# LN1's turned tokens by way of DRAM, in a float32 conditional transformer block on one core

## The chip, the cores and the metric

The kernel runs on one core of a Trainium2 chip. A core has TensorE (PE in the profile: matmuls into PSUM; PEld are its weight loads), VectorE (DVE), ScalarE (ACT), GpSimd (POOL) and SyncE (SP), which here issues nearly all transfers between DRAM and SBUF, the on-chip memory of 128 partitions. Each engine works its own list of instructions in order; semaphores hold an instruction back until what it needs is there. The metric is device time in microseconds, the median of several executions. One execution is also recorded by the hardware profiler; its span runs from the first to the last instruction.

## The reference

Two sequences of 2048 tokens, 512 wide, pass through one block, conditioned on a vector per sequence. Cut to what matters:

```python
emb = jnp.dot(jax.nn.silu(t), ada_w) + ada_b
shift_msa, scale_msa, gate_msa, shift_mlp, scale_mlp, gate_mlp = jnp.split(emb, 6, axis=-1)
norm = _ln(x) * (1.0 + scale_msa[:, None]) + shift_msa[:, None]
h = jax.nn.gelu(jnp.dot(norm, ssm_w1) + ssm_b1, approximate=False)
ssm_out = jnp.dot(h, ssm_w2) + ssm_b2
x = x + gate_msa[:, None] * ssm_out
norm2 = _ln(x) * (1.0 + scale_mlp[:, None]) + shift_mlp[:, None]
hf = jax.nn.gelu(jnp.dot(norm2, ff_w1) + ff_b1, approximate=True)
ff_out = jnp.dot(hf, ff_w2) + ff_b2
x = x + gate_mlp[:, None] * ff_out
```

`ssm_w1` and `ssm_w2` are 512 x 512, `ff_w1` is 512 x 1024 and `ff_w2` 1024 x 512. All of it is float32.

## The kernel before, in words

**Tiling.** The 4096 tokens are cut into 8 blocks of 512 (`NBLK`, `TB`); a block is 1 MB. Blocks 0 to 3 are the first sequence, 4 to 7 the second. The products are done by Strassen's scheme in its Winograd form: an operand is cut in quarters, `first` and `second` (lines 398 and 405) make sums of quarters on VectorE or GpSimd, and seven products take the place of eight, gathered in PSUM banks.

**Stages of a block.** `norm1` (line 562) loads x, normalises each token, turns the block so that channels lie on partitions, scales and shifts it (`modulate`, line 532, four ScalarE instructions) and makes the sums of quarters for the first product (`norm1_sums`, line 542). `ssm1` (line 632) is that product with GELU; `ssm2` (line 675) the second one, added onto x in place and stored to `x1_d` in DRAM. `norm2` (line 598) normalises and turns the result for the feed-forward part and stores it to `turned_d` in DRAM; `tokens` (line 803) reads it back. `ff1` (line 813) and `ff2` (line 899) are the feed-forward part, two blocks at a time. Between them `weight_fw1` (line 722) reads `ff_w1`, makes its sums of quarters and stores them to `fw1_d`, from where `ff1` loads them.

**Turning a block.** `normed` (line 548) takes statistics, normalises (ScalarE) and transposes 32 x 32 squares (`turn`, line 527, VectorE) into one of two buffers in the region `far`, `blocks`. What remains is to exchange groups of 32 partitions. For LN1 that is `move` (line 556): sixteen transfers from SBUF to SBUF of 64 KB each, from 32 partitions of `blocks` to 32 partitions of `turned[i]`. Only after all four transposes can any of them start. Blocks 0 and 1 don't go this way: they are turned on TensorE (`turn_rows`, `rows_normed`), so LN1 by `move` is there for blocks 2 to 7. For LN2, `norm2` writes four times 256 KB into DRAM, each from 32 partitions, at the rows where they belong. In the profile both the moves and these writes are called `turned<-far`; the sizes, 64 and 256 KB, tell them apart.

**Buffers.** `turned[i]` lies in one of two places, by i mod 2, so LN1 of block i may write it only when `ssm1(i - 2)` has read it. `xs[i]` has five places, by i mod 5.

**Order of the work.** The code lists the operations in the order of their data: block i+3's `norm1`, then `ssm2(i)`, `norm2(i)`, `ssm1(i+2)` (lines 1130 to 1141). Class `Plan` (line 18) then fixes the order of each engine's instructions before the program is built. Each operation has a cost on each engine that may do it and a latency. TensorE's order is that of the code. `order` (line 84) works back from TensorE's matmuls to a due time for every operation (`late`); `simulate` (line 107) plays the program forward and gives each free engine, among the operations that can start, the one due soonest. So an engine's order rests on when the plan believes data to be there. On the chip an engine whose next instruction isn't ready waits, with all that stands behind it.

**The plan's DMA.** A transfer takes 640 ns to issue (`ISSUE`). One over 32 KB shares one pipe: it ends at the later of start + 1300 ns (`FLIGHT`) and the pipe's end, plus its bytes at 370 bytes per ns (`RATE`), plus 700 ns (`LANDING`). It may start only when the pipe's end is less than 4000 ns off (`BACKLOG`). For due times, an operation is due its smallest latency plus its bytes at `RATE`, plus 70 ns, before what needs it; `dma` (line 303) has a latency of 2000 ns, and `move` passes one of 2000 + 16 x 640 ns. All transfers of the program but four go by SP's queue, line 308. The framework under the kernel gives each transfer one of the semaphores set aside for DMA in turn, and a transfer whose semaphore is still in use by an earlier one waits at the head of its queue; the old plan doesn't reckon with it.

Of the kernel before, what the change touches and what calls it, by code (L numbers as in the profile page):

```python
# [20 lines left out]
class Plan:  # L21
# [8 lines left out]
    ISSUE, FLIGHT, LANDING, RATE, BACKLOG = 640.0, 1300.0, 700.0, 370.0, 4000.0  # L30
    RATED, LANDED = 0.5, 4000.0
    LITTLE = 1 << 15
    AHEAD, SLACK = 2500.0, 150.0

    def __init__(self, nc):
# [71 lines left out]
    def simulate(self):  # L107
        ops, hop = self.ops, self.HOP
        left, ready = [len(op.deps) for op in ops], [0.0] * len(ops)
        free = dict.fromkeys("pvags", 0.0)  # L110
        self.lock, pipe, holder = 0.0, 0.0, None
        tensor = [op for op in ops if op.engs == "p"]
        at, pools, found = 0, {e: [] for e in "vags"}, {}
        done = [False] * len(ops)

        def enter(op):
            if op.lead and op.late < 1e8:
                ready[op.n] = max(ready[op.n], op.late - op.lead)
            for e in op.engs:
                if e != "p":  # L120
                    pools[e].append(op)
                    found.pop(e, None)

        def choose(e):
            pool = pools[e]
            if not pool:
                return None
            at = {}
            for op in pool:
                wait = self.lock if e in op.shared else pipe - self.BACKLOG if op.size > self.LITTLE else 0.0  # L130
                at[op.n] = max(free[e], ready[op.n], wait)
            now = min(at.values())

            def rank(op):
                return op.late + (self.AHEAD if e == "v" and len(op.engs) > 1 else 0.0), op.n

            op = min((op for op in pool if at[op.n] <= now), key=rank)
            end = now + op.cost[e]
            soon = [u for u in pool if now < at[u.n] < end - self.SLACK and u.late < min(end, op.late)]
            if soon:  # L140
                op = min(soon, key=lambda u: (at[u.n], u.n))
            return at[op.n], op

        for op in ops:
            if not op.deps:
                enter(op)
        count = len(ops)
        while count:
            best = None
            if at < len(tensor) and not left[tensor[at].n]:  # L150
                best = (max(free["p"], ready[tensor[at].n]), -1.0, "p", tensor[at])
            for e in "avgs":
                if e not in found:
                    found[e] = choose(e)
                c = found[e]
                if c and (best is None or (c[0], c[1].late) < best[:2]):
                    best = (c[0], c[1].late, e, c[1])
            start, _, e, op = best
            op.on, op.start, op.after = e, start, None
            free_at, free[e] = free[e], start + op.cost[e]  # L160
            if op.size > self.LITTLE:
                pipe = max(start + self.FLIGHT, pipe) + op.size / self.RATE * (1 + self.RATED * op.care)
                op.end = pipe + self.LANDING + self.LANDED * op.care
                found.pop("a", None), found.pop("s", None)
            else:
                op.end = start + op.lat[e]
                if op.size and e == "s":
                    op.end = max(op.end, pipe + self.LANDING)
            if e in op.shared:
                if e == "g" and holder and holder.on == "v" and start > max(free_at, ready[op.n]):  # L170
                    op.after = holder
                self.lock, holder = start + op.cost[e], op
                found.clear()
            if e == "p":
                at += 1
            else:
                for x in op.engs:
                    pools[x].remove(op)
                    found.pop(x, None)
            count -= 1  # L180
            for s in op.succ:
                o = ops[s]
                gap = 0.0 if o.engs == e and not op.size else hop
                ready[s] = max(ready[s], op.end + gap)
                left[s] -= 1
                if not left[s] and o.engs != "p":
                    enter(o)
# [3 lines left out]
def kernel(  # L191
# [17 lines left out]
    P = 128  # L209
    B, N, D = x.shape  # L210
    H = fw1.shape[1]
    KD, KH = D // P, H // P
    C = 4
    TB = C * P
    HT = TB // 2
    NBLK = B * N // TB
    PER_B = N // TB
    G = 32
# [15 lines left out]
    def cols(ap):  # L234
        n = 1
        for d in ap.shape[1:]:
            n *= d
        return n
# [64 lines left out]
    def dma(o, a, q="s", lead=0.0, lat=2000.0):  # L303
        size = max(cols(o.unsqueeze(0)), 1) * 4
        outs = [o] if o.tensor.name in scratch else []
        ins = [a] if a.tensor.name in scratch else []
        lead = lead or (0.0 if ins or not outs or size <= plan.LITTLE else 25000.0)
        plan.add(q, lambda E: E.dma_start(out=o, in_=a), outs, ins, {q: plan.ISSUE}, {q: lat}, size=size, lead=lead)  # L308
# [19 lines left out]
    def far(name, *shape):  # L328
        t = dram.tile(list(shape), F32, tag=name, name=name)
        scratch.add(t.tensor.name)  # L330
        return t

    def kb(t, at, n):
        return t[:, at * 256 : (at + n) * 256]

    def cut(t, form, **sizes):
        return t.rearrange(form, **sizes)
# [12 lines left out]
        return cut(banks[bank], "p (j t) -> p j t", j=2)  # L350

    x1_d = [far(f"x1_{i}", P, C, D) for i in range(NBLK)]
    turned_d = {i: far(f"turned_{i}", P, C, D) for i in SOON}
    fw1_d = far("fw1_parts", 7, P, 7, W)
    gates_d = {g: far(f"gates_{g}", B, D) for g in (2, 5)}
# [2 lines left out]
    xs = [cut(slots[i % 5], "p (c d) -> p c d", c=C) for i in range(NBLK)]  # L358
    turned = [cut(kb(turned_r, 8 * (i % 2), 8), "p (a r) -> p a r", a=C) for i in range(NBLK)]
# [124 lines left out]
    def stats(xt):  # L484
        t = marks[norms[0] % 4]
        norms[0] += 1
        mv = cut(t[:, :8], "p (c two) -> p c two", c=C)
        for c in range(C):
            st, src, dst = t[:, 8 + 6 * c : 14 + 6 * c], xt[:, c, :], mv[:, c, :]
            plan.add("v", lambda E, st=st, src=src: E.bn_stats(st, src), [st], [src], {"v": 694}, {"v": 680})  # L490
            plan.add("v", lambda E, st=st, dst=dst: E.bn_aggr(dst, st), [dst], [st], {"v": 100}, {"v": 182})
        return t, mv
# [20 lines left out]
    def normal(o, xt, c, rstd, nmr, e="a"):  # L513
        dst, src, b, s = o[:, c, :], xt[:, c, :], nmr[:, c : c + 1], rstd[:, c : c + 1]
        if e == "a":
            act(dst, src, AF.Identity, b, s)
        else:
            plan.add(
                "v",
                lambda E: E.tensor_scalar(dst, src, s, b, ALU.mult, ALU.add),  # L520
                [dst],
                [src, b, s],
                {"v": 560},
                {"v": 640},
            )

    def turn(bl, src, c):
        o = cut(bl, "p (m k c q) -> p k m c q", m=C, k=KD, c=C)[:, :, :, c, :]
        a = cut(src[:, c, :], "p (k m q) -> p k m q", k=KD, m=C)
        plan.add("v", lambda E: E.transpose(o, a), [o], [a], {"v": 636}, {"v": 705})  # L530
# [7 lines left out]
    def next_blocks():  # L538
        turns[0] += 1
        return blocks[turns[0] % 2]  # L540
# [7 lines left out]
    def normed(src, dst, bl, queues="s"):  # L548
        t, mv = stats(src)
        rstd, nmr = scales(t, mv)  # L550
        for c in range(C):
            normal(dst, src, c, rstd, nmr)
            turn(bl, dst, c)
        return cut(bl, "p (m r) -> p m r", m=C)

    def move(to, bl, queues="s"):
        for a in range(C):
            for m in range(C):
                q = queues[m % len(queues)]
                dma(to[m * G : (m + 1) * G, a, :], bl[a * G : (a + 1) * G, m, :], q, lat=2000.0 + 16 * plan.ISSUE / len(queues))  # L560

    def norm1(i, queues="s"):
        plan.stage = f"norm1 {i}"
        load_x(i)
        move(turned[i], normed(xs[i], turned[i], next_blocks()), queues)
        for k in range(KD):
            modulate(turned[i], k, 0, i // PER_B)
        return norm1_sums(i)
# [28 lines left out]

    def norm2(i):
        plan.stage = f"norm2 {i}"
        bl = normed(xs[i], xs[i], next_blocks())  # L600
        for a in range(C):
            dma(turned_d[i][:, a].rearrange("(m q) r -> q m r", m=C), bl[a * G : (a + 1) * G])

# [514 lines left out]
    modulation(3, 1)  # L1120
    plan.care = 0.3
    norm2(0)
    load_ada(5)
    modulation(4, 2)
# [76 lines left out]
```

## Time and profile before

| | us |
|---|---|
| median of 3 runs | 579.64 |
| the three runs | 579.44, 579.64, 582.99 |
| the profiled execution | 580.96 |
| its span | 579.2 |
| its mean granted TensorE clock | 0.996 |
| DMA: 106.96 MB in 49867 packets | queue 1 takes 55.8% of 16 engines' span |

How to read the rows: times are microseconds from the span's start unless ns is said. A window's row gives for each engine its busy time and, behind x, its instructions, then the granted TensorE clock (1.00 is full), the mean busy share of the sixteen DMA engines, and GB/s. A timeline's row gives start, duration, engine, line, operation, what is written <- what is read, how many are merged into the row, and in brackets how long the engine stood idle just before and what released it. A row of waits gives who waited <- for whom, the total, how many times, and the longest. A row of DMA issues gives how many, the size of each and the median time from issue to landing. Every matmul of the code is two records (x) in the profile. TensorE's stages show by their operands: `turned,ring` is `ssm1` up to 200 us and `ff1` from 224 us on, `near,hidden` is `ssm2`.

### The profile page before, as it was taken

How to read it: one execution, taken by the hardware profiler on the slowest of the kernel's cores; microseconds unless marked ns; L12 is line 12 of the kernel's file. 1: busy time of each engine (PE TensorE's matmuls, PEld its weight loads, DVE VectorE, ACT ScalarE, POOL GpSimd, SP SyncE). 2: the span in 40 equal slices, each digit the busy share in tenths (PEclk: the TensorE clock that was granted, in tenths of full speed). 3: DMA queues.
4: the chain of work that ended last, by engine and by line, in shares of the span. 5: the costliest groups of instructions: out<-in, count | busy, mean ns of one | idle time of the engine just before them, and what ended most of it. 6: DMA issues, size and time to landing. Idle time of an engine off the chain costs nothing.

```text
span 579.2 us, 9609 instructions
## 1 busy us (share of the span) xinstructions
PE 567.2 (98%) x3307; PEld 505.6 (87%) x3307; DVE 462.2 (80%) x872; ACT 240.2 (41%) x414; POOL 319.0 (55%) x404
## 2 busy tenths in 40 slices
PE   8999999999998999999999999999999999999997
PEld 5788888888787888888999888999888999888997
DVE  5695865889696688889896789888889997789846
ACT  2463955656384644665202265102255211235010
POOL 1695344889680598976810436711897544336620
PEclk9999999999999999999999999999999999999999
DMA  8953576789578995895034755056846043520022
GB/s 299 392 220 80 185 197 186 220 309 321 175 245 229 346 358 183 314 308 172 30 118 144 236 162 194 23 142 230 296 158 218 1 145 115 195 91 1 2 74 72
DMA packets 49867, 106.96 MB, mean 185 GB/s; under 512 B 6000, under 2 KB 10012, under 8 KB 48924
## 3 DMA queue, kind: packets, MB, share of 16 engines
q1 hardware_dynamic: 49744, 106.34, 55.8%
q8 instruction: 26, 0.43, 0.3%
q14 instruction: 21, 0.17, 0.1%
q10 hardware_dynamic: 76, 0.02, 0.0%
HBM read 68.45 MB, written 31.60 MB: 173 GB/s over the span
## 4 chain that ended last, share of the span: by engine, by line
PE 85%; DMA 5%; POOL 3%; DVE 2%; SPq 2%; issue 1%; ACT 1%; DVEq 0%; ACTq 0%; POOLq 0%
PE bank L286 84%; SPq L308 2%; DMA turned<-far 2%; DMA fw<-in_L_cond_ada_w_dram 1%; DMA ring<-in_L_cond_ssm_w_dram 1%; DMA fw_parts<-fw 1%; POOL near L248 1%; POOL hidden L248 1%; DVE far L530 1%; ACT turned L266 1%; DVE turned L248 0%; POOL fw L248 0%; ACT hidden L266 0%; POOL marks L498 0%; ACT bank L275 0%
## 5 line engine op out<-in xcount | busy, mean ns | idle before, releaser
L286 PE MATMUL bank<-turned,ring 128*128 128x256 f32 x896 | 206.0, 381 | 1.6 <-DMA ring<-in_L_cond_ssm_w_dram 1.3
L286 PEld LDWEIGHTS bank<-turned,ring 128*128 128x128 f32 x896 | 170.2, 191 | 26.3 <-ACT turned L266 1.5
L248 DVE TENSOR_TENSOR hidden<-bank,hidden 128x512 f32<-128x512 f32 (+2 forms) x170 | 125.0, 757 | 41.1 <-PE bank L286 37.4
L248 DVE TENSOR_TENSOR rows<-bank,rows 128x256 f32<-128x256 f32 (+3 forms) x234 | 99.1, 456 | 26.3 <-PE bank L286 19.8
L286 PE MATMUL bank<-near,hidden 128*128 128x256 f32 x448 | 99.9, 382 | 3.8 <-DVE far L248 2.1
L286 PEld LDWEIGHTS bank<-near,hidden 128*128 128x128 f32 x448 | 84.6, 190 | 17.1 <-DVE far L248 2.5
L286 PE MATMUL bank<-ring 128*128 128x256 f32 x336 | 82.2, 381 | 0.0
L286 PE MATMUL bank<-fw,hidden 128*128 128x128 f32 (+1 forms) x512 | 80.1, 301 | 0.0
L286 PEld LDWEIGHTS bank<-fw,hidden 128*128 128x128 f32 x512 | 72.9, 191 | 3.9
L275 ACT COPY bank<-bank 128x512 f32<-128x512 f32 (+2 forms) x67 | 32.3, 482 | 101.4 <-PE bank L286 100.8
L286 PEld LDWEIGHTS bank<-ring 128*128 128x128 f32 x336 | 63.2, 190 | 10.6 <-ACT bank L275 0.8
L248 POOL TENSOR_TENSOR fw<-fw 128x256 f32<-128x256 f32 (+1 forms) x59 | 53.7, 929 | 28.4 <-DMA fw_parts<-fw 12.3
L286 PE MATMUL bank<-fw,far 128*128 128x128 f32 (+2 forms) x624 | 65.8, 286 | 0.3 <-DMA fw<-in_L_cond_ada_w_dram 0.3
L248 POOL TENSOR_TENSOR turned<-turned 128x512 f32<-128x512 f32 (+1 forms) x40 | 45.0, 1140 | 37.9 <-ACT turned L266 17.0
L286 PEld LDWEIGHTS bank<-fw,far 128*128 128x128 f32 (+1 forms) x624 | 59.8, 166 | 3.2 <-issue 1.0
L286 PE MATMUL bank<-fw,near 128*128 128x128 f32 (+1 forms) x432 | 59.5, 290 | 0.0
L286 PEld LDWEIGHTS bank<-fw,near 128*128 128x128 f32 x432 | 54.9, 192 | 1.4
L266 ACT ACTIVATE hidden<-hidden,cols 128x512 f32<-128x512 f32 x64 | 42.6, 714 | 29.3 <-DVE hidden L248 29.1
L266 ACT ACTIVATE turned<-turned,mod,mod 128x512 f32<-128x512 f32 x56 | 41.9, 804 | 21.6 <-DMA turned<-far 10.6
L248 POOL TENSOR_TENSOR hidden<-hidden 128x512 f32<-128x512 f32 (+1 forms) x33 | 40.9, 1243 | 7.1 <-DVE near L248 5.7
L248 POOL TENSOR_TENSOR ring<-turned,ring 128x256 f32<-128x256 f32 x39 | 28.4, 735 | 20.2 <-PE bank L286 13.0
L248 DVE TENSOR_TENSOR turned<-turned 128x512 f32<-128x512 f32 (+1 forms) x52 | 32.2, 642 | 7.3 <-DMA turned<-far 3.9
(102 smaller groups left out, 543.8 us busy)
## 6 DMA issues: line engine op xcount, KB each, us to landing
ring<-fw_parts SPq DMA_DIRECT2D x28, 512.0 KB
ring<-fw_parts SPq DMA_DIRECT2D x28, 384.0 KB, 3.1
turned<-far SPq DMA_DIRECT2D x32, 256.0 KB, 6.1
turned<-turned SPq DMA_DIRECT2D x32, 256.0 KB, 5.9
rows<-x SPq DMA_DIRECT2D x32, 256.0 KB, 4.7
out_dram<-rows SPq DMA_DIRECT2D x30, 256.0 KB, 2.8
fw<-in_L_cond_ada_w_dram SPq DMA_DIRECT2D x6, 1024.0 KB, 11.2
turned<-far SPq DMA_DIRECT2D x96, 64.0 KB, 2.0
```

The lines of the kernel that those rows point to most:

```text
L248: lambda E: E.tensor_tensor(o, a, b, f),
L266: lambda E: E.activation(o, a, func, bias=bias, scale=scale),
L275: plan.add("a", lambda E: E.copy(o, a), [o], [a], {"a": cost}, {"a": cost + 60})
L286: lambda E: E.matmul(o, lhsT, rhs, start=start, stop=stop, skip_group_check=True, **kw),
L308: plan.add(q, lambda E: E.dma_start(out=o, in_=a), outs, ins, {q: plan.ISSUE}, {q: lat}, size=size, lead=lead)
L530: plan.add("v", lambda E: E.transpose(o, a), [o], [a], {"v": 636}, {"v": 705})
```

## The change

Two things. First, LN1 of blocks 3 to 7 no longer uses `move`: the function `turned_out`, taken from the body of `norm2`, writes the turned block to a new DRAM tensor `turned1_d[i]` in four transfers of 256 KB, and one transfer of 1 MB reads it back into `turned[i]`. Block 2 keeps its sixteen moves. The due times of the new transfers use the latency of 2000 ns. Second, the plan keeps the ends of the last eight transfers (`lanes`), and no transfer, of any size and on any queue, is started before the eighth transfer back has ended. A line with a list that nothing used (`done`) is dropped, as are the `queues` arguments of `norm1`. The computation is the same.

```diff
+    LANES = 8
...
-        done = [False] * len(ops)
+        lanes = [0.0] * self.LANES
...
-                at[op.n] = max(free[e], ready[op.n], wait)
+                at[op.n] = max(free[e], ready[op.n], wait, lanes[0] if op.size else 0.0)
...
+            if op.size:
+                lanes = lanes[1:] + [op.end]
+                found.pop("a", None), found.pop("s", None)
...
+    turned1_d = {i: far(f"turned1_{i}", P, C, D) for i in range(3, NBLK)}
...
-    def norm1(i, queues="s"):
+    def turned_out(to, bl):
+        for a in range(C):
+            dma(to[:, a].rearrange("(m q) r -> q m r", m=C), bl[a * G : (a + 1) * G])
+
+    def norm1(i):
         plan.stage = f"norm1 {i}"
         load_x(i)
-        move(turned[i], normed(xs[i], turned[i], next_blocks()), queues)
+        bl = normed(xs[i], turned[i], next_blocks())
+        if i in turned1_d:
+            turned_out(turned1_d[i], bl)
+            dma(turned[i], turned1_d[i])
+        else:
+            move(turned[i], bl)
         for k in range(KD):
             modulate(turned[i], k, 0, i // PER_B)
         return norm1_sums(i)
...
     def norm2(i):
         plan.stage = f"norm2 {i}"
-        bl = normed(xs[i], xs[i], next_blocks())
-        for a in range(C):
-            dma(turned_d[i][:, a].rearrange("(m q) r -> q m r", m=C), bl[a * G : (a + 1) * G])
+        turned_out(turned_d[i], normed(xs[i], xs[i], next_blocks()))
```

## The prediction

> **What bounds the kernel now.** I read the busy times first, then the windows cut at stage borders, then TensorE's waits, then the timeline round each wait.
>
> ```profile
> span 579.2 us, 9609 instructions
> PE 567.2 (98%) x3307; PEld 505.6 (87%) x3307; DVE 462.2 (80%) x872; ACT 240.2 (41%) x414; POOL 319.0 (55%) x404
> ```
> ```profile
> core 0: us, PE busy (x) PEld busy (x) DVE busy (x) ACT busy (x) POOL busy (x), PEclk, DMA share, GB/s
> 0.00:16.00 16.00, 12.35 (x99) 7.33 (x99) 8.86 (x25) 4.78 (x7) 2.76 (x14) 1.00 0.87 307
> 88.00:147.00 59.00, 58.65 (x270) 51.01 (x270) 45.29 (x89) 35.01 (x63) 47.28 (x70) 1.00 0.77 251
> 147.00:188.00 41.00, 37.66 (x169) 32.24 (x168) 30.84 (x58) 22.36 (x38) 20.08 (x36) 0.97 0.73 222
> 266.00:353.00 87.00, 87.00 (x539) 80.09 (x539) 72.23 (x135) 28.43 (x51) 34.14 (x35) 1.00 0.44 145
> 522.00:579.20 57.20, 53.04 (x380) 49.88 (x378) 41.00 (x82) 10.64 (x21) 21.71 (x19) 0.99 0.11 38
> ```
> ```profile
> PE bank L286 <- DVE far L248: 2.1, 1, 2.1
> PE bank L286 <- ACT bank L275: 1.6, 2, 1.2
> PE bank L286 <- DMA ring<-in_L_cond_ssm_w_dram: 1.3, 1, 1.3
> ```
>
> TensorE is the bound: 567.2 of 579.2 us, and no idle time from 266 to 353. The change leaves every matmul as it is, so it can only fill TensorE's 12.0 idle us or add to them. Of these 3.65 lie in the first 16 us and 4.16 after 522 (the end of the last block); 3.34 lie between 147 and 188, inside LN1 of blocks 6 and 7. That is the place to study.
>
> ```profile
> 146.09 1.29 DVE L490 BATCH_NORM_STATS2 marks<-rows 128x6 f32<-128x512 f32 x2 [2.25 <-DMA rows<-in_x_dram]
> 149.59 0.63 ACT L266 ACTIVATE hidden<-hidden 128x512 f32<-128x512 f32 x1 [2.56 <-DVE hidden L248]
> 178.70 2.93 ACT L266 ACTIVATE turned<-turned,mod,mod 128x512 f32<-128x512 f32 x4 [3.79 <-DMA turned<-far]
> 181.72 1.89 DVE L248 TENSOR_TENSOR turned<-turned 128x512 f32<-128x512 f32 x3 [3.93 <-DMA turned<-far]
> ```
> ```profile
> 150.85 8.87 PE L286 MATMUL bank<-near,hidden 128*128 128x256 f32 x40 [1.24 <-ACT bank L275]
> 159.56 12.25 PE L286 MATMUL bank<-turned,ring 128*128 128x256 f32 x56
> 184.27 2.55 PE L286 MATMUL bank<-near,hidden 128*128 128x256 f32 x8 [2.10 <-DVE far L248]
> 186.61 13.43 PE L286 MATMUL bank<-turned,ring 128*128 128x256 f32 x56
> ```
> ```profile
> 186.00:188.00 2.00, 2.00 (x6) 1.56 (x6) 2.00 (x5) 0.59 (x1) 0.00 (x0) 0.50 0.93 294
> ```
>
> Both gaps have one form: an engine works in order and stands at an instruction whose data comes late by DMA, while an instruction that TensorE needs is queued behind it. In the first, VectorE waits 2.25 us for block 7's x, so block 5's hidden values come late, ScalarE's GELU behind them, and ScalarE's copy in a bank behind that: TensorE loses 1.24. In the second, ScalarE waits 3.79 us for block 7's sixteen moves before it modulates, VectorE's LN1 sums wait for ScalarE (the profile names a DMA that landed at about the same moment; the sums read what ScalarE ended at 178.70 + 2.93 = 181.63), and the emptying of ssm2(5)'s bank is queued behind the sums: TensorE loses 2.10. Then the granted clock falls to 0.50, and the next 56 matmul records take 13.43 us where the same stage took 12.25 before: 1.18 more. In all 1.24 + 2.10 + 1.18 = 4.52 us.
>
> On the clock the Trainium skill ("TensorE: Matmul & The Clock Gate", section "Why this matters for your kernels") says that only idle gaps above some 3 us between matmuls bring it down. By that the second gap would be worth 2.10 and not 3.28, and the forecast below 1.18 higher; the trace shows half clock right behind a gap of 2.10, and the measurement decides.
>
> **The change part by part.** *Issues.* Blocks 3 to 7 each lose sixteen moves and gain four writes and a read: 5 x (16 - 5) = 55 issues fewer on SP, and no other queue is touched.
>
> ```profile
> L308 SPq DMA_DIRECT2D turned<-far x128: 303/588/1824, 45.4 to 250.5; - x128
> 106.91 10.02 SPq L308 DMA_DIRECT2D turned<-far  x16
> 163.31 12.15 SPq L308 DMA_DIRECT2D turned<-far  x16
> ```
> ```profile
> 118.61 2.93 ACT L266 ACTIVATE turned<-turned,mod,mod 128x512 f32<-128x512 f32 x4 [0.88 <-DMA turned<-far]
> ```
>
> At the median of 0.588 us they took 55 x 0.588 = 32 us of SP, which has no compute. By itself worth nothing: SP waits elsewhere. What counts is when data lands. Before, from first issue to modulation took 118.61 - 106.91 = 11.7 us (block 5) and 178.70 - 163.31 = 15.4 (block 7).
>
> *The way through DRAM.* The four writes have the form of norm2's, and reads of 1 MB into SBUF are in the profile too.
>
> ```profile
> turned<-far SPq DMA_DIRECT2D x32, 256.0 KB, 6.1
> rows<-in_x_dram SPq DMA_DIRECT2D x3, 1024.0 KB, 9.4
> ring<-in_x_dram SPq DMA_DIRECT2D x2, 1024.0 KB, 5.0
> ring<-in_L_cond_ssm_w_dram SPq DMA_DIRECT2D x1, 1024.0 KB, 6.8
> turned<-far SPq DMA_DIRECT2D x96, 64.0 KB, 2.0
> ```
> ```profile
> turned<-far SPq DMA_DIRECT2D x4, 256.0 KB, 4.3
> ```
> ```profile
> turned<-far SPq DMA_DIRECT2D x8, 256.0 KB, 11.1
> ```
>
> The last two rows are the writes from 62 to 80 and from 120 to 140 us. Three issues stand ahead of the fourth (3 x 0.588 = 1.8), the write lands, the read is issued and lands. Shortest 1.8 + 4.3 + 5.0 = 11.1; longest 1.8 + 11.1 + 9.4 = 22.3; I take the all-run median write and the middle read, 1.8 + 6.1 + 6.8 = 14.7. So data lands no sooner than before (11.7 to 15.4). While the read waits for its writes, all later SP issues stand behind it: x loads, x1 stores, fw1 parts.
>
> The Trainium skill ("DMA: Bandwidth & Descriptors", section "Anatomy of one DMA") gives a transfer about 2.0 us plus bytes at 436 GB/s: an estimate of 2.6 for a write and 4.4 for the read. The way would then be 8.8 us and the forecast 575.1, as in the second case below; medians of 6.1 and 5.0 to 9.4 do not bear that out here, where transfers queue.
>
> *DMA load.*
>
> ```profile
> 45.40:57.00 11.60, 11.60 (x107) 10.21 (x96) 5.63 (x17) 3.48 (x8) 5.99 (x17) 1.00 0.38 92
> 176.20:184.00 7.80, 5.96 (x28) 4.92 (x26) 2.97 (x5) 4.34 (x6) 1.27 (x1) 1.00 0.87 237
> 190.00:192.00 2.00, 2.00 (x11) 1.77 (x10) 2.00 (x4) 2.00 (x4) 0.39 (x1) 1.00 1.07 401
> ```
>
> A block's moves, 1 MB, took 0.38 x 11.6 = 4.4 us of all sixteen DMA engines. In the second row, mostly writes, 1 MB takes about 0.87 x 7.8 / 1.85 MB = 3.7; in the third, mostly reads, 2.7. So a block goes from 4.4 to 6.4, and five add some 10 us of DMA work to the 126 us from 62 to 188, whose share is 0.77 and 0.73 in the rows above from 88 on: near 0.83. Everything that crosses this stretch lands a little later.
>
> *What the plan reckons.* The order of each engine is fixed by the plan, so what matters is how far it misjudges a landing. By its constants sixteen moves take 15 x 0.64 + 1.3 + 0.18 + 0.7 = 11.8 us, the measured ones 11.7 to 15.4: mean lateness about 1.8. For the new way it reckons (1.3 + 4 x 0.71 + 0.7) + (1.3 + 2.83 + 0.7) + 0.07 = 9.7, against my 14.7: lateness 5.0. It also treats LN1's earlier steps as due later: two steps of 4.9 and 2.8 where one of 12.5 was. Extra lateness is 5 x (5.0 - 1.8) = 16 us of waits on ScalarE.
>
> ```profile
> 155.74 2.93 ACT L266 ACTIVATE turned<-turned,mod,mod 128x512 f32<-128x512 f32 x4 [5.04 <-DMA turned<-far]
> 100.95 2.93 ACT L266 ACTIVATE turned<-turned,mod,mod 128x512 f32<-128x512 f32 x4 [0.90 <-DMA turned<-far]
> ```
>
> Before, such waits were 0.88 + 0.90 + 5.04 + 3.79 = 10.6 us, and TensorE lost 2.10 to them, a fifth: block 6's 5.04 cost nothing, as ssm2's banks are emptied by VectorE. A fifth of 16 is 3.2. But LANES works the other way: a plan that holds a transfer back for a free semaphore puts what depends on it later. I take 2.4, between 0 and 3.2.
>
> *The eight semaphores.*
>
> ```profile
> 1.64 7.51 DMA fw<-in_L_cond_ada_w_dram
> 9.17 6.76 DMA ring<-in_L_cond_ssm_w_dram
> ```
>
> They are real: w1's load is the eighth transfer after the first ada_w load, and is issued at 9.17, 0.02 us after that landed. The old plan does not know this. The new one may put w1 ahead of small bias loads; TensorE waits 1.26 for w1 there. Bounds 0 and -1.26; half, -0.63, since the DMA engines are 0.87 busy in that stretch.
>
> **The sum.** The order is new everywhere, so old gaps need not come again. Gap two with its clock goes, -3.28 (bounds 0 and -3.28); gap one half, -0.62 (0 and -1.24), since x lands no sooner but its reader may stand later; the head -0.63; new waits +2.4. Together -2.1. The profiled execution took 580.96 us (span 579.2 and 1.76 round it), 1.32 over the median of 579.64. From the median: **577.5 us**.
>
> **The rivals.** *The way back is short* (11.1 us, near the plan's 9.7): no new waits, 579.64 - 4.53 = 575.1; with the whole first gap and head gone, 573.9. For it: SP is 32 us freer. Against: 9.4 and 11.1 us where DMA is full. *Nothing moves*: gaps fill at one place and open at another, 579.6 (579 to 581.6). For it: LN1 lands no sooner. *Slower: the read comes too late for block 6.* ScalarE's modulation of block 6 ended at 155.74 + 2.93 = 158.67, and TensorE began with it at 159.56, a slack of 0.9. A way of 22.3 is 7.6 longer than 14.7: TensorE stands 6.7 us and loses 1.2 to the clock, 7.9; with block 7 the same, 15.8, and 575.1 + 15.8 = 590.9. It decides against the change once these waits exceed 4.5 us. For it: 0.73 to 0.77 DMA share in those stretches. *The change doesn't do what it says*: TensorE's order is fixed and the transfers are written out, so only the plan's part could be empty; then the head's 0.63 stays, inside the forecast's range.
>
> **How the numbers follow.** About 1% is what a measurement of this kernel can tell from no change: 573.8 to 585.4 us. The forecast (576.3 to 579): 0.36. Short way: 0.28, of it 0.04 under 573.8. Nothing moves: 0.12. Late reads: 0.24, half of it over 585.4. So faster 0.04, same 0.84, slower 0.12. The range 574.2 to 583.5 leaves out about 0.05 below and 0.14 above.
>
> **What would show it.** Right: no 2.10 gap before 184, no 0.50 clock there, ScalarE's wait for turned 3 to 6 us per block from 3 on, DMA share near 0.83 from 62 to 188, TensorE solid from 224. Short way: those waits under 1 us, TensorE idle under 9 us in all. Wrong: a TensorE gap released by ScalarE's modulation or LN1's sums ahead of ssm1(6) or ssm1(7), or one behind an x load that stands in SP's queue after the read.

## The result and the profile after

The kernel after takes 577.59 us (median of 12 runs, 576.23 to 580.65) where the kernel before took 579.92 (12 runs): a ratio of 0.996, 95% interval 0.9942 to 0.9978. The change makes it some 2.3 us faster, and 577.5 was forecast. The steps of the forecast fared worse than its sum.

The page of the kernel after, the span and the engines' line:

```profile
span 576.1 us, 9481 instructions
PE 566.5 (98%) x3307; PEld 504.6 (88%) x3307; DVE 465.4 (81%) x869; ACT 240.3 (42%) x414; POOL 321.2 (56%) x407
```

TensorE now idles 576.1 - 566.5 = 9.6 us, where it idled 12.0. Its windows, cut as before, and behind them the last one's row for the kernel before:

```profile
0.00:16.00 16.00, 14.42 (x105) 8.83 (x106) 8.81 (x25) 4.78 (x7) 4.02 (x14) 1.00 0.90 322
88.00:147.00 59.00, 57.15 (x264) 49.59 (x263) 47.15 (x93) 33.98 (x60) 51.75 (x79) 1.00 0.93 304
147.00:188.00 41.00, 39.56 (x183) 34.20 (x182) 33.26 (x61) 26.60 (x44) 25.80 (x36) 1.00 0.95 312
62.00:188.00 126.00, 122.71 (x565) 106.62 (x564) 98.90 (x188) 80.13 (x138) 91.00 (x131) 1.00 0.92 301
```
```profile
62.00:188.00 126.00, 122.31 (x557) 105.86 (x556) 96.65 (x182) 76.81 (x134) 79.36 (x119) 0.99 0.74 229
```

Of the 2.4 us of idle time less, 2.07 lie in the first 16 us (1.58 where it was 3.65). From 88 to 188 idle time moved rather than went: 147 to 188 has 1.44 us where it had 3.34, but 88 to 147 has 1.85 where it had 0.35. The DMA share from 62 to 188 is 0.92, where it was 0.74. TensorE's timeline, the kernel before's first product and then four rows of the kernel after:

```profile
16.06 7.14 PE L286 MATMUL bank<-turned,ring 128*128 128x256 f32 x32 [1.26 <-DMA ring<-in_L_cond_ssm_w_dram]
```
```profile
14.68 7.44 PE L290 MATMUL bank<-turned,ring 128*128 128x256 f32 x32
99.51 8.95 PE L290 MATMUL bank<-near,hidden 128*128 128x256 f32 x40 [0.43 <-ACT bank L279]
144.42 1.97 PE L290 MATMUL bank<-turned,ring 128*128 128x256 f32 x8 [1.42 <-DVE hidden L252]
184.07 12.63 PE L290 MATMUL bank<-turned,ring 128*128 128x256 f32 x56 [1.43 <-ACT turned L270]
```

The first product begins 1.38 us sooner. The first gap is still there, 1.42 us at 144 in place of 1.24 at 151; the second is 1.43 where it was 2.10, and the clock stays at 1.00 behind it. Behind both stand these rows of VectorE, ScalarE and SP in the kernel after (ScalarE's at 178.89 are block 0's tokens for the feed-forward part, those at 82.03 and 183.21 LN1 of blocks 3 and 7; SP's are block 7's writes, the tokens' reads, block 7's read):

```profile
142.40 1.29 DVE L495 BATCH_NORM_STATS2 marks<-rows 128x6 f32<-128x512 f32 x2 [3.80 <-DMA rows<-in_x_dram]
```
```profile
82.03 2.93 ACT L270 ACTIVATE turned<-turned,mod,mod 128x512 f32<-128x512 f32 x4 [2.68 <-DMA turned<-turned]
178.89 2.93 ACT L270 ACTIVATE turned<-turned,mod,mod 128x512 f32<-128x512 f32 x4 [5.27 <-DMA turned<-turned]
182.26 0.59 ACT L279 COPY bank<-ring 128x512 f32<-128x512 f32 x1 [0.45 <-DVE far L252]
183.21 2.93 ACT L270 ACTIVATE turned<-turned,mod,mod 128x512 f32<-128x512 f32 x4 [0.36 <-DMA turned<-turned]
```
```profile
165.35 2.52 SPq L312 DMA_DIRECT2D turned<-far  x4
168.95 4.04 SPq L312 DMA_DIRECT2D turned<-turned  x4
175.57 0.32 SPq L312 DMA_DIRECT2D turned<-turned  x1
```

Block 7's way from first write to modulation is 183.21 - 165.35 = 17.9 us, where the moves took 15.4, and it begins 2 us later (165.35 against 163.31).

### The profile page after: what moved, and what is told of

Its sections match the earlier page's. It is cut to its first block, busy times and chain, and to the rows that moved or that the text cites. A ratio compares the mean times of both kernels' runs of the same rounds, so it can differ in the third digit from the quotient of the medians.

```text
span 576.1 us, 9481 instructions
## 1 busy us (share of the span) xinstructions
PE 566.5 (98%) x3307; PEld 504.6 (88%) x3307; DVE 465.4 (81%) x869; ACT 240.3 (42%) x414; POOL 321.2 (56%) x407
## 4 chain that ended last, share of the span: by engine, by line
PE 82%; DMA 6%; POOL 4%; DVE 3%; ACT 2%; issue 2%; SPq 1%; DVEq 0%; POOLq 0%
PE bank L290 81%; DMA turned<-turned 3%; POOL fw L252 2%; DMA turned<-far 1%; DMA fw<-in_L_cond_ada_w_dram 1%; DVE hidden L252 1%; ACT turned L270 1%; POOL turned L252 1%; SPq L312 1%; POOL hidden L252 1%; ACT hidden L270 1%; PE bank L300 0%; DMA fw<-in_L_cond_ada_b_dram 0%; DVE far L535 0%; ACT ring L270 0%
## 5 line engine op out<-in xcount | busy, mean ns | idle before, releaser
L290 PE MATMUL bank<-near,hidden 128*128 128x256 f32 x448 | 98.7, 380 | 0.8 <-ACT bank L279 0.4
L252 POOL TENSOR_TENSOR turned<-turned 128x512 f32<-128x512 f32 (+1 forms) x47 | 52.1, 1124 | 25.6 <-ACT turned L270 7.2
L252 POOL TENSOR_TENSOR hidden<-hidden 128x512 f32<-128x512 f32 (+1 forms) x36 | 44.1, 1230 | 27.6 <-ACT hidden L270 17.8
L252 POOL TENSOR_TENSOR fw<-fw 128x256 f32<-128x256 f32 (+1 forms) x54 | 48.4, 914 | 11.8 <-DVE fw L252 8.4
L252 POOL TENSOR_TENSOR ring<-turned 128x256 f32<-128x256 f32 x17 | 12.4, 728 | 53.9 <-PE bank L290 51.1
L252 POOL TENSOR_TENSOR ring<-turned,ring 128x256 f32<-128x256 f32 x36 | 26.8, 746 | 13.5 <-PE bank L290 9.4
```

The costliest lines, as they stand in the source:

```text
L252: lambda E: E.tensor_tensor(o, a, b, f),
L290: lambda E: E.matmul(o, lhsT, rhs, start=start, stop=stop, skip_group_check=True, **kw),
```

## The experiments

Theories at the start. *Head and plan*: the gain is w1's earlier load and what the plan does with it; the way through DRAM is no gain by itself. Rival, *the way*: the transfers carry the gain. Some kernels hold an order that was planned: the plan runs as it is, and afterwards either only the transfers are exchanged, or a few operations are put at another place of the sorted list, with what depends on them; the rest keeps its order.

Each kernel is set against runs of the kernel before on the same chip. The rows come from several chips, so from row to row the ratios are the safer comparison. The last column is TensorE's idle time from 40 to 266 us in the profiled execution (226 less the busy time of the windows 40 to 88, 88 to 147, 147 to 188 and 188 to 266).

| kernel | us | ratio, interval | idle, us |
|---|---|---|---|
| before | 579.1 to 579.9 | 1 | 3.70 |
| after | 577.59 | 0.996, 0.9942 to 0.9978 | 3.30 |
| plan_only | 574.64 | 0.9915, 0.9902 to 0.9927 | 0.43 |
| route_only | 580.19 | 1.0011, 0.9986 to 1.0035 | 2.13 |
| w1_first | 578.92 | 0.9994, 0.9973 to 1.0014 | 3.51 |
| route_in_old_order | 574.15 | 0.9906, 0.9893 to 0.9919 | 0.35 |
| due_as_before | 575.10 | 0.9935, 0.9915 to 0.9954 | 1.01 |
| landing_as_measured | 590.55 | 1.0208, 1.0183 to 1.0232 | 12.21 |
| read_ahead_of_tokens | 577.33 | 0.9967, 0.9946 to 0.9988 | 2.43 |
| route_in_plan_only_order | 573.28 | 0.9905, 0.9886 to 0.9925 | 0.01 |
| moves_due_late | 576.51 | 0.9941, 0.9918 to 0.9965 | 1.88 |
| due_and_landing | 579.96 | 0.9998, 0.9974 to 1.0021 | 4.31 |
| issues_kept | 586.43 | 1.0108, 1.0069 to 1.0147 | 11.58 |
| statistics_later | 576.72 | 0.995, 0.9929 to 0.9971 | 1.67 |

The times are medians, the idle times are from one execution: that of route_only (577.95 us) lies 2.2 us below its median, and that of issues_kept (588.89) 2.5 above.

**plan_only.** The second half of the change alone.

```diff
-    turned1_d = {i: far(f"turned1_{i}", P, C, D) for i in range(3, NBLK)}
+    turned1_d = {i: far(f"turned1_{i}", P, C, D) for i in ()}
```

> The plan reckons with eight semaphores, and LN1 keeps its sixteen moves in every block. Theory (head and plan): ssm1(0) begins at 14.7 us where it began at 16.06, and most of that reaches the end, so 578.5 us with 577 to 580, by how the two gaps between 147 and 188 us turn out. Rival (the way through DRAM carries the gain): ssm1(0) may begin sooner, but the gaps of block 7 stay and the time is 579.9 as before.

574.64 us: better than the whole change, and below the theory's range. The new order puts block 7's moves three us sooner than before, and both gaps go. SP's row for them:

```profile
160.25 10.35 SPq L312 DMA_DIRECT2D turned<-far  x16
```

**route_only.** The first half alone.

```diff
-                at[op.n] = max(free[e], ready[op.n], wait, lanes[0] if op.size else 0.0)
+                at[op.n] = max(free[e], ready[op.n], wait)
```

> LN1 of blocks 3 to 7 goes by DRAM, and the plan does not know of the semaphores. Theory (head and plan): ssm1(0) begins at 16.06 as before, ScalarE waits for the read back 3 us or more in several blocks, since nothing holds the plan's reading of it back, and the time is 579.9 with 578.5 to 583. Rival (the way through DRAM carries the gain): 577.6 as with both parts.

580.19 us, no difference from before that can be told: inside the theory's range, against the rival. But the reason given for it does not hold: only one block's modulation waits over 1 us for its read (2.34, block 3). What the kernel loses in its median is not in this profile: its mean clock is 1.000, while eight of the twelve runs show 0.994 to 0.997.

**w1_first.** The order before, held, but for one load.

```diff
+    early = ada_load.start + 1.0
...
-    for op in plan.order():
+    for op in shifted(ops, lambda op: early if op is w1_load else op.start):
```

> The kernel before with its old order on every engine, except that w1's load is issued right behind the second ada_w load, ahead of six loads of 1 KB. Theory: the head's 1.1 to 1.4 us is this one place in SP's queue, ssm1(0) begins at about 14.7, the later gaps stay, 578.7 us. Rival: later waits swallow it, 579.9.

The first product begins at 14.78 us as expected, but the time is 578.92 with an interval on both sides of 1. Of the head's 1.3 us no gain is shown; two gaps, of 1.46 and 1.16 us, stand at 182 and 189 in its profile.

**route_in_old_order.** The order before, held; only the transfers are exchanged.

```diff
...
+                if by is not None:
+                    plan.ops[-1].fn = lambda E: None
+                    n = C * a + m
+                    if n < C:
+                        row = by[:, n].rearrange("(m q) r -> q m r", m=C)
+                        plan.ops[-1].fn = lambda E, o=row, n=n: E.dma_start(out=o, in_=bl[n * G : (n + 1) * G])
+                    elif n == C * C - 1:
+                        plan.ops[-1].fn = lambda E: E.dma_start(out=to, in_=by)
```

> The kernel before with its old order on every engine, and in SP's queue the sixteen moves of blocks 3 to 7 replaced by four writes at the places of the first four and the read at the place of the last; the order was planned with moves. Theory: the way through DRAM is itself no gain, data lands 1 to 4 us later (15 to 18 us from first issue to modulation where it was 11.7 to 15.4), ScalarE's waits for turned grow from 10.6 us to 15 or more and the gap before 184 us with them, 581 to 585 us. Rival (SP's 55 issues fewer are the gain): data lands sooner, the gap shrinks, under 579.

574.15 us, against the theory, and with it falls the step of the prediction on which the theory stood. ScalarE's modulation of blocks 6 and 7, and block 7's transfers on SP:

```profile
152.56 2.93 ACT L266 ACTIVATE turned<-turned,mod,mod 128x512 f32<-128x512 f32 x4 [5.81 <-DMA turned<-turned]
173.35 2.93 ACT L266 ACTIVATE turned<-turned,mod,mod 128x512 f32<-128x512 f32 x4 [2.36 <-DMA turned<-turned]
```
```profile
159.46 4.05 SPq L567 DMA_DIRECT2D turned<-far  x4
166.99 0.34 SPq L569 DMA_DIRECT2D turned<-turned  x1
```

The way is 173.35 - 159.46 = 13.9 us, close to the 14.7 that I estimated. What I missed is the first column: in the same order block 7's transfers begin at 159.46 where the moves began at 163.31. SP is through sooner with all that stands before them, x loads included, and no wait of VectorE for block 7's x is left. In its head the first product also begins sooner, at 15.12, with the order there unchanged. It begins at 14.95 in issues_kept and at 16.09 in route_only, where that order is the old one too, and w1's load is issued between 9.12 and 9.23 us in all of these and in the kernel before. So one execution's head says little about the order there; why w1 lands at different times stays open.

**issues_kept.** The test of that reading: as above, but the eleven places left empty get small transfers.

```diff
...
+                    else:
+                        plan.ops[-1].fn = lambda E, o=small_d[by.tensor.name][n], n=n: E.dma_start(out=o, in_=bl[:G, 0, :G])
```

> As route_in_old_order, with the eleven places of the moves that fell away filled by small extra transfers of 4 KB from the turned block to a DRAM tensor that nothing reads, so SP issues sixteen again and one read. Theory (SP's queue: fewer issues is what the way through DRAM saves): the read is issued some 7 us later, x loads and stores behind it too, 578.5 us (577 to 581). Rival (the transfers themselves are quicker than sixteen moves): 574.2 as without them.

586.43 us: the direction of the theory, but 12.3 us above route_in_old_order where 4.3 was expected. SP's rows for block 7, ScalarE's modulation, and the gap:

```profile
168.67 4.85 SPq L568 DMA_DIRECT2D turned<-far  x4
173.56 6.07 SPq L572 DMA_DIRECT2D small<-far  x11
179.74 0.36 SPq L570 DMA_DIRECT2D turned<-turned  x1
```
```profile
186.43 2.93 ACT L266 ACTIVATE turned<-turned,mod,mod 128x512 f32<-128x512 f32 x4 [6.28 <-DMA turned<-turned]
```
```profile
192.00 3.45 PE L286 MATMUL bank<-near,hidden 128*128 128x256 f32 x8 [3.98 <-DVE far L248]
```

Eleven issues take 6.07 us, the read stands behind them, and the way is 17.8 us. Without these issues the way through DRAM is 5.5 us faster than the moves, with them 6.6 us slower, so what it saves goes with the eleven issues fewer per block. How much of the 12.3 us is SP's time alone is not shown: the small transfers also move data and take semaphores, and block 7's first write, 5.4 us later than the first move in the kernel before, stands behind TensorE gaps of 2.31 and 2.72 us in earlier blocks.

**due_as_before.** Why do the halves not add up? One number in the kernel after.

```diff
-            dma(turned[i], turned1_d[i])
+            dma(turned[i], turned1_d[i], lat=2000.0 + 4800.0)
```

> The kernel after, with one number changed: the read back counts 6800 ns instead of 2000 in the due times, so LN1's steps up to the turning are due as early as with sixteen moves; the plan's reckoned landing stays. Theory (due times): block 7's writes are issued near 160 us where they were at 165.35, the gap ahead of ssm1(7) goes, 574.5 us (574 to 576). Rival (landing misjudged): ScalarE and SP still count on data after 9.7 us, the two gaps stay, 577.6.

575.10 us, inside the range of the due times' theory, and below all twelve runs of the kernel after; the intervals of the two ratios overlap a little. Block 7's writes begin at 162.2 us, three sooner than in the kernel after, though not at 160 (three writes of LN2 stand before them). VectorE no longer waits for block 7's x, so the gap at 144 us is gone. The gap ahead of ssm1(7), of which the theory said that it goes, is still there, 0.99 where it was 1.43. ScalarE's modulation of block 7 doesn't wait for its read; it stands behind a copy that does wait:

```profile
181.20 12.63 PE L290 MATMUL bank<-turned,ring 128*128 128x256 f32 x56 [0.99 <-ACT turned L270]
```
```profile
179.81 0.59 ACT L279 COPY bank<-ring 128x512 f32<-128x512 f32 x1 [1.60 <-DVE far L252]
180.34 2.93 ACT L270 ACTIVATE turned<-turned,mod,mod 128x512 f32<-128x512 f32 x4
```

**landing_as_measured.** The other number instead.

```diff
+            plan.slow.update({n: 1500.0, n + 1: 1500.0, n + 2: 1500.0, n + 3: 1500.0, n + 4: 3500.0})
...
-                op.end = pipe + self.LANDING + self.LANDED * op.care
+                op.end = pipe + self.LANDING + self.LANDED * op.care + self.slow.get(op.n, 0.0)
```

> The kernel after, with the plan's reckoned landing of LN1's writes 1.5 us later and of the read 3.5 us later, 14.7 us in all where it was 9.7; the due times stay. Theory (due times): LN1 of block 7 still begins late, 577.6 us. Rival (landing misjudged): what reads turned stands later in the queues, the gap ahead of ssm1(7) shrinks, 575 us (574 to 576.5).

590.55 us, far off both. With a landing nearer the truth and due times that don't cover it, the plan finds an order in which block 7's writes come at 171.56, six us later than in the kernel after. Why it finds that one is not shown.

**due_and_landing.** Both numbers.

> The kernel after with both numbers changed: 6800 ns for the read in the due times, and the reckoned landing 5 us later in all. Theory (the due times have to cover the reckoned landing): with 12.5 us of due time against 14.7 of landing nearly all of the 590.6 goes away, 575.5 us (574 to 578). Rival (a later reckoned landing does the harm whatever the due times): above 584.

579.96 us, a miss of both: better than 590.55 by 10.6, so the due times do most, but not the 575.5 expected. A gap of 3.34 us stands ahead of ssm1(7). Block 7's writes are issued at 161.00 and its read only at 172.02, behind three writes of LN2, but the read is not what the gap waits for at the end. ScalarE's modulation follows a copy without a wait of its own, and the copy waited for VectorE to empty ssm2's bank:

```profile
184.41 0.59 ACT L279 COPY bank<-ring 128x512 f32<-128x512 f32 x1 [10.27 <-DVE far L252]
184.94 2.92 ACT L270 ACTIVATE turned<-turned,mod,mod 128x512 f32<-128x512 f32 x4
```

An order that rests on truer landings is not the better order here.

**moves_due_late.** The due times from the other side: plan_only, with LN1 due 4.8 us later.

```diff
-                dma(..., lat=2000.0 + 16 * plan.ISSUE / len(queues))
+                dma(..., lat=2000.0 + 16 * plan.ISSUE / len(queues) - (4800.0 if to is not turned[2] else 0.0))
```

> As plan_only (eight semaphores in the plan, sixteen moves in every block), but the moves of blocks 3 to 7 count 7440 ns instead of 12240 in the due times, so LN1 is due 4.8 us later there, as it is in the kernel after. Theory (due times): LN1 of block 7 begins later, its moves after 163 us, a gap comes back ahead of ssm1(6) or ssm1(7), 577.5 us (576 to 581). Rival (the due times cost only where the way goes through DRAM): 574.6 as plan_only.

576.51 us, 1.9 over plan_only, at the low end of the range (the intervals of the two ratios touch). SP and TensorE in it:

```profile
163.41 16.11 SPq L312 DMA_DIRECT2D turned<-far  x20
```
```profile
158.06 12.63 PE L290 MATMUL bank<-turned,ring 128*128 128x256 f32 x56 [1.86 <-DMA fw_parts<-fw]
```

Block 7's moves are back where they were before, and a gap is back ahead of ssm1(6). The transfer that the row names is no operand of ssm1; the modulation of block 6, on ScalarE from 157.21, is.

**read_ahead_of_tokens.** The order after, held; the tokens of block 0 stand behind block 7's LN1.

```diff
...
+    read = max(op.start for op in ops if op.note == "norm1 7" and op.on == "s")
+    first = min(op.start for op in ops if op.note == "tokens 0")
...
-    for op in plan.order():
+    for op in shifted(ops, lambda op: op.start + (read + 10.0 - first + (0.0 if op.on == "s" else 4000.0) if op.note == "tokens 0" else 0.0)):
```

> The kernel after with its order held, except that block 0's tokens for the feed-forward part (four reads, their modulation and sums) stand behind block 7's read and modulation. Both theories take the gap of 1.43 us ahead of ssm1(7) for a read that is issued late: it goes with its 0.38 of slower matmuls, 575.8 us. Rival: the writes' landing holds the read back and not its place in SP's queue; then the gap stays, 577.6.

577.33 us; the gap is 1.14 where it was 1.43. The rival holds for SP: the read is issued at 173.60, only 2 us sooner, as it has to wait for its writes. And ScalarE shows a second cause that neither theory had:

```profile
181.58 0.59 ACT L279 COPY bank<-ring 128x512 f32<-128x512 f32 x1 [8.78 <-DVE far L252]
182.10 2.93 ACT L270 ACTIVATE turned<-turned,mod,mod 128x512 f32<-128x512 f32 x4
```

The copy that fills ssm2's next bank has to wait until ssm2(5) has been emptied from it, and the modulation of block 7 stands behind the copy. In plan_only and route_in_old_order LN1 comes soon enough to stand ahead of it (172.11 and 173.35).

**statistics_later.** The order after, held; VectorE's statistics of block 7 stand later.

```diff
...
-    for op in plan.order():
+    for op in shifted(ops, lambda op: op.start + (4000.0 if op.note == "norm1 7" and op.on == "v" and op.cost["v"] in (694, 100) else 0.0)):
```

> The kernel after with its order held, except that block 7's four pairs of statistics on VectorE stand up to 4 us later, behind the two additions from PSUM that TensorE needs. Theory: the gap of 1.42 us at 144 us is VectorE standing at statistics whose x has not landed; it goes, 576.2 us. Rival: the statistics move the gap to ssm1(7), 577.6.

The gap at 144 us is gone in its profile, and no wait for block 7's x is left, so its cause is shown. What it costs is not shown: in time 576.72 is 0.9 below the kernel after, with intervals that overlap, and a new gap of 0.56 stands at 160.

**route_in_plan_only_order.** The best order with the best transfers: plan_only's order, held, with the exchange of route_in_old_order.

> The order planned with eight semaphores and sixteen moves, held on every engine; in SP's queue the moves of blocks 3 to 7 are replaced by four writes and a read. Theory: each part takes the same idle time of TensorE away, so together they give no more than the better one, 573.9 us (573 to 574.7). Rival (the parts disturb each other on the chip, not in the plan): 577 as with both parts planned.

573.28 us, as the theory had it: the lowest here, 4.3 below the kernel after, with an interval that overlaps those of plan_only and route_in_old_order. The whole list of TensorE's waits in it:

```profile
PE bank L290 <- POOL far masks.py:199: 1.3, 1, 1.3
PE bank L290 <- POOL near L252: 0.4, 1, 0.4
```

Nothing is left between 40 and 266 us, so on the chip the halves do not disturb each other; they do so in the plan. Of the 4.3 us the due times account by the medians for some 2.5 (due_as_before); where the other 1.8 come from stays open.

## Why the prediction came out right, and where it did not

*The bound: right.* TensorE's idle time moved (12.0 to 9.6 us), its busy time by 0.7 only, which is less than the half clock had cost, and in the table the kernels with little idle time take the least time.

*Gap two and the clock, -3.28: too large.* The 2.10 and the half clock went; 1.43 came at the same place. I had the new idle time in another term. And 1.18 of it should not have been taken from the median: it is the half clock of the profiled execution, whose mean clock is 0.996. Of the 69 runs of the kernel before beside the experiments, 54 show 0.998 or more.

*Gap one, -0.62: wrong.* It is 0.18 larger, for the same reason, and statistics_later shows that reason.

*The head, -0.63: not shown.* The first product begins 1.38 us sooner in the profile, a little over the bound of 1.26. But with the old order there it began anywhere from 14.95 to 16.09, and w1_first shows no gain in the end from the head alone.

*New waits, +2.4: about the size, not the cause.* TensorE's new gaps are 0.43 and 1.43. I had priced them by 16 us more of ScalarE's waits for a read that the plan counts on too soon; ScalarE waited 2.68 and 0.36 us for LN1's reads, less than the 10.6 before. The longest wait, 5.27, is for another stage's tokens. What costs, as far as the runs tell, is that LN1 begins late. I had named that ("treats LN1's earlier steps as due later") and given it no price: due_as_before puts it at 2.5 us by the medians, moves_due_late at 1.9, and in both the intervals of the ratios still meet.

*The issues, "by itself worth nothing": wrong, and the largest error.* SP does no compute, but its queue stands ahead of x loads and LN1's transfers. In the old order held the exchange is worth 5.5 us, and with the issues put back it costs 6.6. In plan_only's order, which has little idle time left to fill, it is worth some 1.4, with intervals that overlap. The Trainium skill ("DMA: Bandwidth & Descriptors", section "Issuing engines are not separate DMA queues") calls the time to initiate a DMA "usually small relative to the DMA itself". For one transfer that is so here: 0.588 us to issue, and 2.0 from issue to landing for a move of 64 KB. In a queue it misleads: eleven issues took 6.07 us, nearly as long as the 6.7 from the issue of the read behind them to its use.

*DMA share near 0.83: too low.* It is 0.92. The 1 MB reads took 8.6 us at the median where I took 6.8. The shorter way of 8.8 us, which I estimated from the Trainium skill ("DMA: Bandwidth & Descriptors", section "Anatomy of one DMA"), was not seen either: block 7's took 13.9 in route_in_old_order, and the page gives its figure for transfers that GpSimd issues, while these are SP's.

So the sum was right while its parts were not, and that is partly luck. Measured, the new plan alone takes 5.0 us (579.66 to 574.64, plan_only), where my terms for the old gaps, the clock and the head came to 4.53 with 1.18 of them misplaced. The way through DRAM, planned on its short due times, gives 2.95 back (574.64 to 577.59), where I had 2.4 for reads that come late. That it is planned so, and not the transfers themselves, is what costs: in the same order held they cost nothing (573.28). The rival "the way back is short" came nearer on waits for the reads, 2.68 us and less, but not on the length of the way, 17.9 us for block 7, nor on the plan.

## What to carry to other kernels

A queue that does no compute is still a place where work stands in line: count its issues ahead of the transfer that the bound engine waits for. Where a planner fixes the order, judge a change of transfers twice, once in the old order held and once replanned; here the same exchange gave -5.5 us in the old order and nothing that can be told when the old plan was run again for it. A cheaper transfer also changes what the planner thinks is urgent; look at the due times before the landing times.

## What the runs showed of the hardware that was not expected

The clock does not follow the length of a gap alone. Gaps of 2.10 us in the kernel before and of 2.68 in landing_as_measured (ended at 86.27) were followed by half clock; the gap of 2.72 us in issues_kept (ended at 111.74) and that of 3.34 in due_and_landing (ended at 185.80) were not. TensorE's row behind the second, whose 56 records take 12.63 us at full clock, and then the windows that hold the last two, issues_kept first:

```profile
86.27 13.94 PE L290 MATMUL bank<-turned,ring 128*128 128x256 f32 x56 [2.68 <-ACT turned L270]
```
```profile
110.00:114.00 4.00, 2.26 (x11) 2.01 (x11) 3.97 (x7) 2.27 (x4) 4.00 (x4) 1.00 0.99 285
192.00:194.00 2.00, 2.00 (x6) 1.60 (x7) 2.00 (x4) 0.23 (x1) 0.00 (x0) 0.59 0.95 340
```
```profile
186.00:188.00 2.00, 1.99 (x9) 1.44 (x9) 1.56 (x4) 1.86 (x3) 0.00 (x0) 1.00 0.95 283
```

The gap of 3.98 us ended at 192.00 and brought the clock to 0.59 in the next 2 us. One and the same kernel also differs from execution to execution: of due_and_landing's twelve runs three have a mean clock of 1.000 and take 577.6 to 577.8 us, eight have 0.996 or 0.997 and take 579.2 to 581.6. So a price for the clock that is read from one profile need not be the median's.

The Trainium skill ("TensorE: Matmul & The Clock Gate", section "What's actually happening") speaks of a window of about 3.4 us that runs on by itself. The gap of 3.34 that does not cost, and the differences between executions, would fit a window with its own start. Gaps of 2.10 and 2.68 that do cost are shorter than the window and would fit only if one that is idle in part can count; no run here shows that, nor where the windows begin. The limit of some 3 us that the prediction quotes is not a limit here.
